# Fixed rotation of four score banks, and another order of score units, in an attention and mixture-of-experts kernel

## Chip, cores and metric

The kernel runs on one core of one Trainium2 chip. The metric is the device time of one execution in microseconds; less is better. Three runs of the kernel before took 604.11, 605.59 and 605.93 us, a median of 605.59.

## What is computed

A pre-norm transformer layer: causal attention with 16 heads of 8 values, then a mixture of 8 experts of which each token uses 2. The input is 8 sequences of 512 tokens with 128 values, all in float32.

```python
x = x + attn(layernorm(x))
x = x + moe(layernorm(x))

def attn(x):                        # b=8, t=512, H=16, HD=8
    q, k, v = (x @ Wq), (x @ Wk), (x @ Wv)      # split into heads
    s = einsum('bqhd,bkhd->bhqk', q * HD**-0.5, k)
    p = softmax(where(causal, s, -inf))
    return einsum('bhqk,bkhd->bqhd', p, v) @ Wo + bo

def moe(x):                         # E=8, F=512, TOPK=2
    probs = softmax(x @ gate_w.T)
    topk_probs, topk_idx = top_k(probs, 2)
    hidden = relu(einsum('th,ehf->tef', x, w1) + b1)
    all_out = einsum('tef,efh->teh', hidden, w2) + b2
    return sum(all_out[topk_idx] * topk_probs)
```

## The kernel before

The program is recorded by a set of Python generators ("lanes": setup, project, shifts, attend, route, experts, sums). Each yields a number, the point in time at which its next piece should be recorded, in units of one sequence; the lane with the least number goes on (L1351 to L1359). For PE, ACT, DVE and SP the order of recording is the order on the engine. So each of these engines works through one fixed list, and an instruction that waits holds up all behind it on its engine.

Attention computes its scores twice. A tile of scores is always 128 partitions by 512 float32, one PSUM bank.

The lane `shifts` (L557) finds the largest score of each row. For a group of four heads (two pairs of heads, `pr`) it goes through three kinds of unit, `S_UNITS` (L83): kind 0 has two banks, kind 1 two banks, kind 2 one. Each bank gets its causal blocks by bfloat16 matmuls (L597 for the blocks left of the diagonal, L602 for the diagonal one), and VectorE takes the maximum over it (L616) into `pm`. After the six units of a group, the maxima are combined and negated (`nm`, L622), split into two bfloat16 parts (`nh`, L632 and L633), and, two units into the next group, transposed by PE (`nmTp`, L562), copied by ACT (`nmT`, L564) and written by two POOL DMAs as two more rows of `q2` (L570). With those rows, the second pass gives scores from which the row's maximum has been taken.

The lane `attend` (L642) makes the second pass, key-major, some two groups behind `shifts` (LEAD, 0.55 of a sequence). `T_UNITS` (L88) has two kinds with two banks and one with one; per group there are six units, of 2, 2, 2, 2, 1 and 1 banks. Each bank is filled by L752 and L757 and read by one exp on ACT (L762) into `pt`. The exps are later multiplied by the values (`po`, L673). In the recorded order a unit of `attend` is followed by a unit of `shifts`, in turn; a group has ten banks of each. Other lanes put their work in between: projections of a later sequence (L446 to L458), norms and routing of an earlier one, and expert tiles (`ph` L1251, ReLU L1258 or L1260, `py` L1110, L1114).

PSUM has eight banks: `ps_sc` (L123) holds four for the scores of both passes, and, behind attention, for `ph` of the expert tiles; `ps_mm` three for everything else; `ps_o` one for `po`. In `ps_sc` all tiles carry one tag, so a new tile takes whichever of the four buffers the tile framework picks when the program is built. A tile's first matmul waits until the reader of the bank's last tile has finished.

Of the kernel before, what the change touches and what calls it, by code (L numbers as in the profile page):

```python
# [9 lines left out]
F32 = mybir.dt.float32  # L10
# [3 lines left out]
ALU = mybir.AluOpType  # L14
AX = mybir.AxisListType
PSUM = bass.MemoryType.PSUM
# [10 lines left out]
def preln_attn_moe(ctx: ExitStack, tc: tile.TileContext, x, wq, wk, wv, wo, bo,  # L27
# [57 lines left out]
        (((0, 0, 0), (0, 2, P)), ((1, 0, 0), (1, 2, P))),  # L85
        (((0, 1, 0), (1, 1, 2 * P)),),
    )
    T_UNITS = (  # L88
        (((0, 0, 0),), ((1, 0, 0),)),
        (((0, 1, 0), (0, 3, 3 * P)), ((1, 1, 0), (1, 3, 3 * P))),  # L90
# [29 lines left out]
    work = ctx.enter_context(tc.tile_pool(name="work", bufs=2))  # L120
    small = ctx.enter_context(tc.tile_pool(name="small", bufs=2))
    slots = ctx.enter_context(tc.tile_pool(name="slots", bufs=1, space=DRAM))
    ps_sc = ctx.enter_context(tc.tile_pool(name="ps_sc", bufs=4, space=PSUM))  # L123
    ps_mm = ctx.enter_context(tc.tile_pool(name="ps_mm", bufs=3, space=PSUM))
    ps_o = ctx.enter_context(tc.tile_pool(name="ps_o", bufs=1, space=PSUM))

# [129 lines left out]
    def in_order(ins):  # L256
        tc.keep_in_program_order(ins)
        if last_exp[0] is not None:
            tc.add_manual_dep(
                ins.ins, last_exp[0].ins.name,  # L260
                mybir.DependencyInfo(
                    mybir.DependencyClass.Sync, mybir.DependencyReason.DATA
                ),
                reason="indirect transfers keep the pace of attention",
            )

    def mm_tile(name):
        return ps_mm.tile([P, T], F32, tag="mm", name=name)
# [288 lines left out]
    def shifts():  # L557
        late = []

        def transposed(b, g, nh):  # L560
            pt = mm_tile(f"nmTp_{b}_{g}").bitcast(BF16)
            nc.tensor.transpose(pt[:, :P], nh, ident_bf)  # L562
            nmT = small.tile([32, P], BF16, tag="nmT", name=f"nmT_{b}_{g}")
            nc.scalar.copy(nmT, pt[:32, :P])  # L564
            late.append(lambda: rows(b, g, nmT))

        def rows(b, g, nmT):

            for l in range(2):
                ins = nc.gpsimd.dma_start(  # L570
                    out=q2_buf[b % 2][KS + l : KS + l + 1, HG * g : HG * g + HG],
                    in_=nmT[16 * l : 16 * l + 16],
                )
                if b > 0:
                    tc.keep_in_program_order(ins)
            shifted.add((b, g, 2))

        for b in range(B):
            for g in range(G):
                t0 = b - LEAD + g / G + (0.1 if b == 0 < g else 0.0)  # L580
                yield t0
                assert b in packed
                q2, k2 = q2_buf[b % 2], k2_buf[b % 2]

                pm = pm_buf[g % 2].rearrange("p (n u) t k -> p u n (t k)", u=2)
                for pr in range(2):
                    n = 2 * g + pr
                    for i, unit in enumerate(S_UNITS):
                        yield t0 + (3 * pr + i) / 24
                        for v, bank in enumerate(unit):  # L590
                            ps = ps_sc.tile(
                                [P, T], F32, tag="sc", name=f"s_{b}_{n}_{i}_{v}"
                            )
                            for u, t, at in bank:
                                h, q = 2 * n + u, ts(t, P)
                                if t > 0:
                                    nc.tensor.matmul(  # L597
                                        ps[:, at : at + t * P], lhsT=q2[:KS, h, q],
                                        rhs=k2[:KS, h, : t * P],
                                        start=(at == 0), stop=True, skip_group_check=True,  # L600
                                    )
                                nc.tensor.matmul(  # L602
                                    ps[:, at + t * P : at + (t + 1) * P],
                                    lhsT=q2[:, h, q], rhs=k2[:, h, q],
                                    start=(at + t == 0), stop=True, skip_group_check=True,
                                )
                            blocks = ps.rearrange("p (a q) -> p a q", q=P)
                            if i == 0:
                                top, src = pm[:, v, pr, 12:13], ps
                            elif i == 1:  # L610
                                top, src = pm[:, v, pr, 3:7], blocks
                            else:
                                top, src = pm[:, :, pr, 8], ps.rearrange(
                                    "p (u k) -> p u k", u=2
                                )
                            nc.vector.tensor_reduce(top, src, AX.X, ALU.max)  # L616
                        if t0 + (3 * pr + i) / 24 < 0:
                            keep_warm(WARM[2], f"{g}_{pr}_{i}")
                        if late:
                            late.pop(0)()  # L620
                nm = small.tile([P, HG * NT], F32, tag="nm", name=f"nm_{b}_{g}")
                nc.vector.tensor_reduce(  # L622
                    nm, pm_buf[g % 2].rearrange("p h t k -> p (h t) k"), AX.X, ALU.max,
                    negate=True,
                )
                nh = nh_buf[g % 2]
                nm = nm.rearrange("p (h o a) -> p h o a", o=2, a=2)
                hi, lo = (
                    nh[:, ts(l, HG * NT)].rearrange("p (h a o) -> p h o a", a=2, o=2)
                    for l in range(2)  # L630
                )
                V.tensor_copy(hi, nm)  # L632
                V.tensor_tensor(lo, nm, hi, ALU.subtract)  # L633
                if b > 0:
                    late.append(lambda: None)
                late.append(lambda b=b, g=g, nh=nh: transposed(b, g, nh))
        while late:
            late.pop(0)()
            yield B - LEAD + 0.05


    def attend():  # L642
# [90 lines left out]
        for b in range(B):  # L733
            for g in range(G):
                yield b + g / G
                assert (b, g, 2) in shifted
                q2, k2 = q2_buf[b % 2], k2_buf[b % 2]
                for i, unit in enumerate(T_UNITS):
                    pts = []
                    for pr in range(2):  # L740
                        yield b + g / G + (2 * i + pr + 0.5) / 24
                        n = 2 * g + pr
                        pt = work.tile(
                            [P, 2, T], F32, tag="pt", name=f"pt_{b}_{n}_{i}", bufs=6
                        )
                        for v, bank in enumerate(unit):
                            ps = ps_sc.tile(
                                [P, T], F32, tag="sc", name=f"st_{b}_{n}_{i}_{v}"
                            )
                            for u, j, at in bank:  # L750
                                h, k = 2 * n + u, ts(j, P)
                                nc.tensor.matmul(  # L752
                                    ps[:, at : at + P], lhsT=k2[:, h, k], rhs=q2[:, h, k],
                                    start=(at == 0), stop=True, skip_group_check=True,
                                )
                                if j < NT - 1:
                                    nc.tensor.matmul(  # L757
                                        ps[:, at + P : at + T - j * P],
                                        lhsT=k2[:KO, h, k], rhs=q2[:KO, h, (j + 1) * P :],
                                        start=False, stop=True, skip_group_check=True,  # L760
                                    )
                            last_exp[0] = nc.scalar.activation(pt[:, v, :], ps, AF.Exp, scale=SCALE)  # L762
                        pts.append(pt)
                        go_on()
                    products.append(lambda b=b, g=g, pts=pts, unit=unit, i=i: product(
                        b, g, pts, unit, i == 0, i == 2))
                attended.add((b, g))
# [279 lines left out]
    def experts():  # L1047
# [192 lines left out]
        for n, (s, i) in enumerate(tiles):  # L1240
            first, m = quad(s, i)
            yield when(s, i + 1)
            if after(s, i):
                ph = ps_sc.tile([P, T], F32, tag="sc", name=f"ph_{s}_{i}")
                hT = work.tile([P, 2, T], F32, tag="pt", name=f"hT_{s}_{i}", bufs=6)
                hT = hT[:, 0, :].rearrange("p (c t) -> p c t", c=FC)
            else:
                ph = mm_tile(f"ph_{s}_{i}")
                hT = work.tile([P, FC, P], F32, tag="hT", name=f"hT_{s}_{i}")
# [138 lines left out]
```

## Time and profile before

| | |
|---|---|
| median of three runs | 605.59 us |
| the profiled execution | 598.14 us |
| its span, first to last instruction | 596.4 us |
| mean granted TensorE clock | 0.954 |
| PE busy (share of the span) | 515.4 us (86%) |
| PE weight loads | 378.0 us (63%) |
| DVE | 430.9 us (72%) |
| ACT | 306.5 us (51%) |
| POOL | 220.2 us (37%) |
| L762, exp, 320 of 128x512 | 179.1 us, 600 ns each |
| L616, maximum, 320 of 128x512 | 206.0 us, 682 ns each |

Engines are PE (TensorE matmuls), PEld (its weight loads, which overlap them), DVE (VectorE), ACT (ScalarE), POOL (GpSimd) and SP (SyncE). Busy time is the time in which an instruction of the engine is in flight; matmuls are pipelined, so a new one may start while an older one's record still runs. Where a row has an arrow and a name behind idle time, that instruction's end is what released the waiting one. In names such as `pt<-st`, the left side is written and the right side read; L762 is line 762 of the kernel. Score matmuls of the first pass (tile `s`) run from 25.7 to 428.7 us, those of the second (tile `st`) from 44.9 to 462.5 us.

### The profile page before, as it was taken

To read this page: it belongs to the slowest core of one execution; us is meant where nothing else is said; L and a number is where in the kernel's file an instruction comes from. 1 tells how busy PE (TensorE), PEld (TensorE's weight loads), DVE (VectorE), ACT (ScalarE), POOL (GpSimd) and SP (SyncE) were. 2 spreads that over 40 slices of the span, in tenths; PEclk is the share of its full clock that TensorE was granted. 3 is DMA by queue.
4 is the path that set the end of the run, shared out by engine and by line. 5 is a ranking of instruction groups with operands and counts; after the bars stand their busy time and mean duration, and the time that the engine had idled before them with its cause. 6 is when DMAs were issued, how large, how long until landed. Compare 5 with 4: busy or idle time off the path is not lost. (4 is left out here: it accounts for less than half of the span.)

```text
span 596.4 us, 14010 instructions
## 1 busy us (share of the span) xinstructions
PE 515.4 (86%) x4762; PEld 378.0 (63%) x4762; DVE 430.9 (72%) x1367; ACT 306.5 (51%) x673; POOL 220.2 (37%) x278
## 2 busy tenths in 40 slices
PE   6979999988888988888799999998899788879980
PEld 4745455545445565665566777766576687879970
DVE  7788778898778977978788877797753354323694
ACT  2646656665645566465447465654454233345530
POOL 4032202315514422533443336335335334654441
PEclk9888899999979999999799999999999788999995
DMA  2568198188199455406502784322344586668783
GB/s 57 160 133 186 28 226 210 38 214 215 27 208 181 125 142 127 124 19 179 149 30 67 180 202 120 89 64 73 87 116 114 181 248 185 192 184 246 243 293 110
DMA packets 68762, 86.07 MB, mean 144 GB/s; under 512 B 11540, under 2 KB 50748, under 8 KB 66652
## 3 DMA queue, kind: packets, MB, share of 16 engines
q1 hardware_dynamic: 61508, 74.87, 49.1%
q0 software_dynamic: 6592, 9.65, 5.0%
q8 instruction: 39, 0.64, 0.5%
q10 hardware_dynamic: 592, 0.66, 0.4%
q14 instruction: 31, 0.25, 0.2%
HBM read 61.34 MB, written 26.16 MB: 147 GB/s over the span
## 5 line engine op out<-in xcount | busy, mean ns | idle before, releaser
L762 ACT ACTIVATE pt<-st 128x512 f32<-128x512 f32 x320 | 179.1, 600 | 128.1 <-PE st L752 58.3
L616 DVE TENSOR_REDUCE pm<-s 128x1 f32<-128x512 f32 (+2 forms) x320 | 206.0, 682 | 36.4 <-PE s L602 30.3
L1148 POOL DMA_INDIRECT ys<-yo,to x78 | 76.1, 975 | 125.4 <-ACT pt L762 50.2
L597 PE MATMUL s<-k,q 72*128 72x384 bf16 (+2 forms) x384 | 93.9, 280 | 16.0 <-ACT pt L762 12.8
L752 PE MATMUL st<-q,k 128*128 128x128 bf16 x512 | 92.9, 222 | 14.8 <-ACT pt L762 6.4
L602 PE MATMUL s<-k,q 128*128 128x128 bf16 x512 | 94.3, 223 | 7.4 <-ACT pt L762 5.5
L757 PE MATMUL st<-q,k 74*128 74x256 bf16 (+2 forms) x384 | 93.9, 280 | 0.0
L673 PE MATMUL po<-pt,va 128*18 128x512 f32 (+3 forms) x1024 | 92.5, 445 | 0.5 <-ACT pt L762 0.3
L1110 PE MATMUL py<-w_sb,hT 128*128 x624 | 88.6, 286 | 4.2 <-DVE yo L1114 2.0
L1016 POOL DMA_INDIRECT xs<-xn_f,slot x64 | 63.2, 987 | 64.1 <-ACT pt L762 35.7
L1110 PEld LDWEIGHTS py<-w_sb,hT 128*128 128x128 f32 x624 | 79.5, 199 | 8.2 <-issue 3.6
L602 PEld LDWEIGHTS <-q 128*128 128x128 bf16 x512 | 51.0, 100 | 37.7 <-issue 34.8
L570 POOL DMA_DIRECT2D q<-nmT x64 | 33.7, 529 | 76.4 <-ACT nmT L564 71.1
L597 PEld LDWEIGHTS <-q 72*128 72x128 bf16 x384 | 37.8, 100 | 36.5 <-issue 29.7
L752 PEld LDWEIGHTS <-k 128*128 128x128 bf16 x512 | 51.6, 101 | 6.3 <-issue 2.4
L757 PEld LDWEIGHTS <-k 74*128 74x128 bf16 x384 | 37.7, 98 | 26.2 <-issue 20.8
L673 PEld LDWEIGHTS po<-pt,va 128*18 128x18 f32 x1024 | 23.1, 97 | 29.6 <-issue 22.7
L1251 PE MATMUL ph<-xgT,wt 128*128 128x128 f32 x288 | 41.0, 286 | 0.8 <-ACT pt L762 0.8
L1251 PEld LDWEIGHTS ph<-xgT,wt 128*128 128x128 f32 x288 | 35.8, 195 | 5.7 <-issue 2.4
L1258 ACT ACTIVATE hT<-ph,q 128x128 f32<-128x128 f32 x72 | 21.0, 368 | 27.9 <-PE ph L1251 11.7
L1258 ACT ACTIVATE hT<-ph,wt 128x128 f32<-128x128 f32 x72 | 20.6, 367 | 22.3 <-issue 10.9
L456 POOL TENSOR_TENSOR part<-rest,part 128x512 bf16<-128x512 f32 x14 | 16.2, 1162 | 41.6 <-issue 33.8
(172 smaller groups left out, 688.0 us busy)
## 6 DMA issues: line engine op xcount, KB each, us to landing
wt<-wrows SPq DMA_DIRECT2D x36, 322.0 KB
k<-kparts SPq DMA_DIRECT2D x42, 192.0 KB
q<-wrows SPq DMA_DIRECT2D x24, 322.0 KB
k<-wrows SPq DMA_DIRECT2D x18, 322.0 KB
q<-qparts SPq DMA_DIRECT2D x30, 192.0 KB
q<-ys SPq DMA_DIRECT2D x15, 256.0 KB
k<-xs SPq DMA_DIRECT2D x42, 65.0 KB
qparts<-part SPq DMA_DIRECT2D x14, 192.0 KB
```

What stands on the lines that cost most here:

```text
L597: nc.tensor.matmul(ps[:, at : at + t * P], lhsT=q2[:KS, h, q], rhs=k2[:KS, h, : t * P], start=(at == 0), stop=True, skip_group_check=True,)
L602: nc.tensor.matmul(ps[:, at + t * P : at + (t + 1) * P], lhsT=q2[:, h, q], rhs=k2[:, h, q], start=(at + t == 0), stop=True, skip_group_che ...
L616: nc.vector.tensor_reduce(top, src, AX.X, ALU.max)
L673: nc.tensor.matmul(po[32 * h : 32 * h + 2 * VC, j * P :], lhsT=va[:, j, c0 : c0 + 2 * VC], rhs=at_cols(pts[pr], unit, u, at, W), start=(fi ...
L752: nc.tensor.matmul(ps[:, at : at + P], lhsT=k2[:, h, k], rhs=q2[:, h, k], start=(at == 0), stop=True, skip_group_check=True,)
L757: nc.tensor.matmul(ps[:, at + P : at + T - j * P], lhsT=k2[:KO, h, k], rhs=q2[:KO, h, (j + 1) * P :], start=False, stop=True, skip_group_c ...
L762: last_exp[0] = nc.scalar.activation(pt[:, v, :], ps, AF.Exp, scale=SCALE)
L1016: ins = nc.gpsimd.indirect_dma_start(out=xs[k], out_offset=bass.IndirectOffsetOnAxis(ap=slot[b][:, j * NT + i : j * NT + i + 1], axis=0), ...
L1110: nc.tensor.matmul(py, lhsT=hT[:, c, :], rhs=w2_sb[:, bass.ds(at[s, i] + c * E * D, D)], start=(c == 0), stop=(c == FC - 1),)
L1148: ins = nc.gpsimd.indirect_dma_start(out=ys[k], out_offset=bass.IndirectOffsetOnAxis(ap=to[s, first][:, i - first : i - first + 1], axis=0 ...
L1251: nc.tensor.matmul(ph[:, ts(c, P)], lhsT=wt[s, i][:, ts(c, P)], rhs=turned[s, first][:, ts(i - first, P)], start=True, stop=True,)
L1258: nc.scalar.activation(hT[:, c, :], ph[:, ts(c, P)], AF.Relu, bias=bias)
```

## The change

The pool of the score banks keeps four buffers, but as four tags of one buffer each, and a counter gives them out in turn: 1, 2, 3, 0, 1 and so on, over both passes and the expert tiles behind attention. The six units of a group in `shifts` are no longer recorded pair by pair (two banks, two, one, two, two, one) but in the order of `S_ORDER`, whose entries are (kind, pair): two banks, one, two, one, two, two. What each unit does is unchanged, and so are the points in time at which units are recorded.

```diff
+    S_ORDER = ((0, 0), (2, 0), (1, 0), (2, 1), (0, 1), (1, 1))
...
-    ps_sc = ctx.enter_context(tc.tile_pool(name="ps_sc", bufs=4, space=PSUM))
+    ps_sc = ctx.enter_context(tc.tile_pool(name="ps_sc", bufs=1, space=PSUM))
...
+    turn = [0]
+
+    def score_tile(name):
+        turn[0] = (turn[0] + 1) % 4
+        return ps_sc.tile([P, T], F32, tag=f"sc{turn[0]}", name=name)
...
-                for pr in range(2):
-                    n = 2 * g + pr
-                    for i, unit in enumerate(S_UNITS):
-                        yield t0 + (3 * pr + i) / 24
-                        for v, bank in enumerate(unit):
-                            ps = ps_sc.tile(
-                                [P, T], F32, tag="sc", name=f"s_{b}_{n}_{i}_{v}"
-                            )
+                for m, (i, pr) in enumerate(S_ORDER):
+                    n, unit = 2 * g + pr, S_UNITS[i]
+                    yield t0 + m / 24
+                    for v, bank in enumerate(unit):
+                        ps = score_tile(f"s_{b}_{n}_{i}_{v}")
...
-                            ps = ps_sc.tile(
-                                [P, T], F32, tag="sc", name=f"st_{b}_{n}_{i}_{v}"
-                            )
+                            ps = score_tile(f"st_{b}_{n}_{i}_{v}")
...
-                ph = ps_sc.tile([P, T], F32, tag="sc", name=f"ph_{s}_{i}")
+                ph = score_tile(f"ph_{s}_{i}")
```

More of the change, by code (lines that the diff above doesn't have):

```diff
@@ L585, in shifts @@
                 pm = pm_buf[g % 2].rearrange("p (n u) t k -> p u n (t k)", u=2)
-                for pr in range(2):
-                    n = 2 * g + pr
-                    for i, unit in enumerate(S_UNITS):
-                        yield t0 + (3 * pr + i) / 24
-                        for v, bank in enumerate(unit):
-                            ps = ps_sc.tile(
-                                [P, T], F32, tag="sc", name=f"s_{b}_{n}_{i}_{v}"
-                            )
[L594 to L600, printed above, removed]
-                                    )
[L602 to L605, printed above, removed]
-                                )
[L607 to L620, printed above, removed]
@@ new lines, in shifts @@
+                for m, (i, pr) in enumerate(S_ORDER):
[3 more added lines that the diff above has]
+                        ps = score_tile(f"s_{b}_{n}_{i}_{v}")
+                        for u, t, at in bank:
+                            h, q = 2 * n + u, ts(t, P)
+                            if t > 0:
+                                nc.tensor.matmul(
+                                    ps[:, at : at + t * P], lhsT=q2[:KS, h, q],
+                                    rhs=k2[:KS, h, : t * P],
+                                    start=(at == 0), stop=True, skip_group_check=True,
+                                )
+                            nc.tensor.matmul(
+                                ps[:, at + t * P : at + (t + 1) * P],
+                                lhsT=q2[:, h, q], rhs=k2[:, h, q],
+                                start=(at + t == 0), stop=True, skip_group_check=True,
+                            )
+                        blocks = ps.rearrange("p (a q) -> p a q", q=P)
+                        if i == 0:
+                            top, src = pm[:, v, pr, 12:13], ps
+                        elif i == 1:
+                            top, src = pm[:, v, pr, 3:7], blocks
+                        else:
+                            top, src = pm[:, :, pr, 8], ps.rearrange(
+                                "p (u k) -> p u k", u=2
+                            )
+                        nc.vector.tensor_reduce(top, src, AX.X, ALU.max)
+                    if t0 + m / 24 < 0:
+                        keep_warm(WARM[2], f"{g}_{pr}_{i}")
+                    if late:
+                        late.pop(0)()
@@ L746, in attend @@
                         for v, bank in enumerate(unit):
-                            ps = ps_sc.tile(
-                                [P, T], F32, tag="sc", name=f"st_{b}_{n}_{i}_{v}"
-                            )
+                            ps = score_tile(f"st_{b}_{n}_{i}_{v}")
                             for u, j, at in bank:
```

## The prediction

> **What bounds the kernel now.** First the table of busy time by stretch, split where attention's scores begin (45 us) and end (430 us) and where the last exp has run (463 us); columns are PE, PEld, DVE, ACT, POOL busy us, then granted clock:
>
> ```profile
> 45.00:430.00 385.00, 346.30 (x3412) 230.31 (x3410) 316.21 (x922) 221.05 (x454) 137.11 (x162) 0.97 0.52 127
> 430.00:463.00 33.00, 30.84 (x291) 23.35 (x283) 15.84 (x79) 17.36 (x43) 12.59 (x14) 1.00 0.44 120
> 463.00:597.00 134.00, 103.53 (x827) 98.87 (x827) 64.21 (x278) 47.14 (x151) 57.82 (x60) 0.89 0.69 209
> ```
>
> The change works in the first row, 385 us. PE looks 90% busy there, DVE 82% (316/385), ACT 57%. The chain of waits covers only the last 130 us (expert matmuls behind attention, which the change leaves alone), so I read the first stretch from the waits inside it:
>
> ```profile
> ACT pt L762 <- PE st L752: 55.3, 47, 2.9
> DVE pm L616 <- PE s L602: 25.8, 37, 1.8
> PE s L597 <- ACT pt L762: 12.8, 23, 2.4
> PE st L752 <- ACT pt L762: 6.4, 12, 1.0
> PE s L602 <- ACT pt L762: 5.5, 9, 1.6
> PE st L752 <- DVE pm L616: 3.3, 7, 1.0
> ```
>
> Columns: total us, times, longest. PE waits 24.7 us for exps (12.8+6.4+5.5, 44 times) and 5.1 us for maxima (with 0.9+0.9 of L597 and L602), and the readers wait for PE in turn. So PE, in program order, is the pacemaker, and what holds it up is a score bank that has not been read yet.
>
> These totals understate it, because a matmul's record is 0.22 us long while the next may start 0.06 us later: shorter holds don't show as idle. The timeline has one of each sort:
>
> ```profile
> 219.54 0.22 PE L757 MATMUL st<-q,k 74*128 74x128 bf16 x1
> ...
> 219.77 0.22 PE L602 MATMUL s<-k,q 128*128 128x128 bf16 x1
> 219.86 0.60 ACT L762 ACTIVATE pt<-st 128x512 f32<-128x512 f32 x1 [1.05 <-PE st L757]
> 220.51 0.22 PE L602 MATMUL s<-k,q 128*128 128x128 bf16 x1 [0.52 <-ACT pt L762]
> ```
>
> ```profile
> 160.39 0.22 PE L602 MATMUL s<-k,q 128*128 128x128 bf16 x1
> ...
> 160.64 0.69 DVE L616 TENSOR_REDUCE pm<-s 128x2 f32<-128x512 f32 x1 [0.59 <-PE s L602]
> ...
> 161.05 0.22 PE L602 MATMUL s<-k,q 128*128 128x128 bf16 x1
> 161.39 0.32 PE L597 MATMUL s<-k,q 72*128 72x384 bf16 x1
> ```
>
> From the last matmul into a bank to the first of its next tile takes 0.97 us through an exp (219.54 to 220.51) and 1.00 us through a maximum (160.39 to 161.39), with the reader idle. One bank of scores takes PE 0.22 us (a 384-column record is followed after 0.165, a 128-column one after 0.056). In the first case PE had one bank to fill in between and stood still from 219.83 to 220.51; in the second it lost 0.28 us (161.05+0.06 to 161.39) and the waits view shows nothing.
>
> **The holds, counted.** I laid the score tiles' bank addresses, as built, beside the records of L597, L602, L752, L757 and their readers L616, L762. A hold is a first matmul that starts later than the pitch of the matmul before it allows, within 0.15 us of its bank's read ending. Over the kernel they make 58.5 us: 44.9 behind exps, 13.6 behind maxima. Sorted by "cover", PE's bare matmul time between the two uses of the bank:
> behind exps, cover under 0.6 us: 87 uses, 40.3 us; longer cover: 239 uses, 4.6 us;
> behind maxima, cover under 0.8 us: 26 uses, 4.0 us; longer cover: 294 uses, 9.6 us.
>
> **Part one: banks in turn.** Before, of 678 reuses 6 come one score tile later (the second bank of a unit on the bank of its first), 87 two, 117 three, 265 four, 203 five to seven. After, the built program has 678 at four. Counting cover along its PE order, with the same pitches: exps 0 under 0.6 and 316 above; maxima 88 under 0.8 (all 0.67 to 0.74, three banks of 0.22) and 232 above. Prices of the long classes as measured, class by class: 6.2 us for exps, 8.4 us for maxima. The first class, 40.3 us, goes. What is new is that 88 times, not 26, PE meets a bank whose maximum has had only three banks of time.
>
> **The price of those 88** was bounded from three rows. Least: the 26 of before cost 4.0/26 = 0.15 us; but 20 of them had DVE idle (turnaround 1.00), having fallen there by choice. Most: the first maximum of most units ends on average 1.43 us after the last matmul into its bank started (records of L616 against L597/L602), so 1.43+0.05-0.06-0.67 = 0.75 us. Between: with DVE idle the first bank of a unit costs 1.00-0.06-0.67 = 0.27, and the second, whose maximum comes 0.61 after the first (two in 1.29 us) while PE needs only 0.22, another 0.39; mean 0.33. A third of first maxima start at once. I take 0.40, nearest to the idle case, because a PE held up by DVE gives DVE time to catch up. 88 x 0.40 = 35.2 us.
>
> Sum for the banks: 6.2 + 8.4 + 35.2 = 49.8 against 58.5: -8.7 us. With 0.15: 27.8, -30.7. With 0.75: 80.6, +22.1.
>
> **Part two: the order of units.** The same 10 banks, 28 matmuls and 10 maxima per group of four heads; the orders of ACT and SP do not change, PE's and DVE's only inside the score units. A group now ends on a two-bank unit: its second maximum ends about 0.61 us later, and with it nm and nh (L622 to L633). In the next group one bank fewer stands ahead of the transposition L562, 0.22 us. Queued behind that are the next exp tile's matmuls on PE. Its slack, from the end of nh to L562, was below 0.9 us in 7 of 32 groups (0.66, 0.15, 0.06, 0.06, 0.38, 0.65, 0.44). If all were lost that is 3.9 us; where PE waits for maxima anyway the two overlap. I take +2 (0 to 3.9). The row copies on POOL and the exps behind them have two groups of lead, the cover that keeps them free: some 25 us (L597 and L602 run from 25.7 to 428.9 us, 12.6 for each of 32 groups). Were that gone, the one wait of st for nmT's rows, 1.8 us, is the price.
>
> **The clock.** Granted clock is 0.66 in two 10-us stretches of attention (170 to 180, 290 to 300) and 1.00 nearly everywhere else there: some 3.4 us of PE time each. One more or one fewer moves the time by that much either way; it goes into the range.
> The Trainium skill, "TensorE: Matmul & The Clock Gate", section "A second HAM failure mode: psum-queue depth-cycling", speaks against the change: cycling through banks with small pauses between the matmuls made the clock swing between half and full. By the row nothing is added; by the rule, more such stretches, an estimate of one or two at the row's 3.4 us, which would turn the sum to about 0. No run here shows it yet.
>
> **The sum.** -8.7 + 2 = -6.7 us. On the profiled execution: 598.14 us (span 596.4 and 1.7 around it) becomes 591.4. The median of the three runs, 605.59, lies 7.45 above the profile; moved by the same amount it gives **598.9 us**.
>
> **Rivals.**
> 1. *DVE is the wrong engine to wait for* (slower). The waits move from ACT, 57% busy, to DVE, 82% busy. Three times a group (two before a score unit, one before the first exp tile) PE comes back 0.67 to 0.74 us after filling a bank that waits in DVE's queue behind norms, routing and ReLUs. For: mean end 1.43 us, and 1.97 for the unit that follows another closely. Against: the holds behind maxima are only 13.6 us now, and such a hold never leaves DVE idle. It decides from 58.5 = 14.6 + 2 + 88p, p = 0.48 us. At 0.60 it gives 605.59+10.9 = 616.5; at the bound 0.75, 629.7.
> 2. *The short waits cost little* (much faster): at the idle-DVE price for a first bank, 0.27, holds are 38.4: -20.1, 585.5; at 0.15 and no transposition loss, 574.9. For: the measured 0.15. Against: those uses were not placed blindly.
> 3. *Nothing comes through*: PE's gain is spent at the next thing in line (oqp, expert weights, DVE's 82%), 605.6.
> 4. *It doesn't do what it says*: excluded, the built addresses are at distance four throughout.
>
> **How the numbers follow.** Forecast 0.32 (own range 592 to 603), rival 2 0.20, rival 3 0.11, rival 1 0.37. Range: down to 582 (leaves out about half of rival 2's lower part, 0.07), up to 618 (leaves out a third of rival 1, 0.12). About 0.3%, 1.8 us, is what these runs can tell from no change. Faster 0.52, same 0.11, slower 0.37.
>
> **What would show it.** Right: PE's waits for exps fall from 24.7 us to under 5, the 0.52-like gaps after T tiles vanish, and waits of s and st on L616 rise from 5.1 us, not above 20; attention's last exp ends 5 to 10 us before 463. Wrong: waits for L616 above 30 us, or the end of attention unmoved while exp waits vanish (rival 3), or a third stretch at clock 0.66.

## The result, and the profile after

| | before | changed |
|---|---|---|
| median of 20 runs each, beside each other | 604.29 us (597.99 to 609.09) | 603.48 us (602.22 to 610.76) |
| mean of the 20 | 604.40 | 604.64 |
| ratio to before, 95% interval | | 1.007 (1.0041 to 1.010) |
| the profiled execution, its span | 598.14, 596.4 | 610.76, 609.0 |
| its mean granted clock | 0.954 | 0.933 |

The forecast gain of 6.7 us is not there. The ratio leaves out runs more than 1.5% above a kernel's fastest one, and as one run of before at 597.99 us puts that bar at 606.96, six of before's 20 fall out (607.16 to 609.09) and none of the changed kernel's, which is why the ratio says 0.7% slower where means and medians agree. Two later comparisons of the same changed kernel gave 0.995 (0.9893 to 1.0006) and 1.0045 (0.9996 to 1.0095), and before against itself 1.0035 (0.9986 to 1.0085). It is a change of nothing, or of some 2 us for the worse.

The table of busy time by stretch of the changed kernel, at the same bounds as before (us, then PE, PEld, DVE, ACT, POOL busy, granted clock, DMA share, GB/s):

```profile
45.00:430.00 385.00, 346.15 (x3358) 228.34 (x3359) 312.80 (x915) 215.67 (x448) 133.53 (x158) 0.96 0.52 125
430.00:463.00 33.00, 29.67 (x248) 21.70 (x248) 16.89 (x76) 15.78 (x37) 10.43 (x13) 0.84 0.37 101
463.00:597.00 134.00, 114.80 (x919) 107.62 (x917) 63.71 (x280) 52.62 (x162) 62.43 (x66) 0.93 0.68 208
```

In the first 385 us PE is as busy as before (346.15 against 346.30 us) but shows 3358 matmuls instead of 3412, so it runs late by some 50 matmuls, in part because of its clock (0.96 against 0.97). The second row has a clock of 0.84 where before had 1.00. In the third PE does 919 matmuls instead of 827: the end is the same work, met later.

PE's waits in attention (45 to 440 us) of the changed kernel; total us, times, longest:

```profile
PE st L755 <- DVE pm L621: 11.9, 33, 1.4
PE s L607 <- DVE pm L621: 10.1, 24, 1.1
PE s L602 <- DVE pm L621: 7.5, 11, 1.5
PE st L755 <- ACT pt L765: 1.9, 6, 0.5
PE nmTp L570 <- DVE nh L638: 1.6, 1, 1.6
```

L602, L607, L755 are the old L597, L602, L752; L621 is the maximum (old L616), L765 the exp (old L762), L570 the transposition (old L562). The change does what it says: waits for exps have gone from 24.7 to 1.9 us. What the first three lines say is where they went: 29.5 us behind maxima, from 5.1.

Counted with the shorter holds, as in the prediction (us that a first matmul of a score tile starts late behind its bank's reader):

| holds, us | behind exps | behind maxima | all |
|---|---|---|---|
| before, first profile and second | 44.9, 44.6 | 13.6, 14.8 | 58.5, 59.4 |
| changed, three profiles | 4.6, 5.0, 3.9 | 52.0, 52.5, 53.1 | 56.6, 57.5, 56.9 |

Nearly all that was saved behind exps is paid again behind maxima. One such hold, in the timeline of the changed kernel (start, duration, both us; in brackets the idle time before, and what ended it):

```profile
184.75 0.34 PE L602 MATMUL s<-k,q 72*128 72x384 bf16 x1
...
184.93 0.22 PE L607 MATMUL s<-k,q 128*128 128x128 bf16 x1
...
185.01 0.18 DVE L638 TENSOR_TENSOR nh<-nm,nh 128x16 bf16<-128x16 f32 x1
185.10 0.16 DVE L929 TENSOR_SCALAR have<-pc 128x8 int32<-128x8 f32 x1
...
185.67 0.22 PE L570 MATMUL nmTp<-ident_bf,nh 128*128 128x128 bf16 x1
...
186.43 0.17 DVE L956 TENSOR_TENSOR steps<-begins 128x8 f32<-128x8 f32 x1
186.51 1.28 DVE L621 TENSOR_REDUCE pm<-s 128x1 f32<-128x512 f32 x2
...
187.19 0.60 ACT L765 ACTIVATE pt<-st 128x512 f32<-128x512 f32 x1 [2.81 <-PE nmTp L570]
187.25 0.22 PE L755 MATMUL st<-q,k 128*128 128x128 bf16 x1 [1.36 <-DVE pm L621]
```

PE fills the bank by 184.93, fills three more, does a transposition at 185.67 and is back at the bank in turn. Its maximum has not begun: on DVE, routing's small operations (L929 to L956, 0.15 to 0.21 us each) stand ahead of it until 186.51. PE stands still until 187.25, with everything behind it. In this hold no other bank would have served: the other three are read out later, one by the exp at 187.19 (until 187.79), two by maxima (until 187.79 and 189.04). In others one would. Comparing, at each hold behind a maximum, the ends of the reads of all four banks gives 23.5, 24.6 and 24.2 us in the three profiles of the changed kernel, of 52 to 53, that went by after another bank was free; in before it is 1 us of 14 to 15.

### The profile page after: what moved, and what is told of

Same layout as the page of the kernel before. It is cut to its first block, busy times and chain, and to the rows that moved or that the text cites. A ratio compares the mean times of both kernels' runs of the same rounds, so it can differ in the third digit from the quotient of the medians.

```text
span 609.0 us, 14013 instructions
## 1 busy us (share of the span) xinstructions
PE 526.6 (86%) x4762; PEld 383.2 (63%) x4762; DVE 430.8 (71%) x1367; ACT 304.8 (50%) x673; POOL 220.1 (36%) x278
## 4 chain that ended last, share of the span: by engine, by line
PE 50%; DVE 32%; issue 7%; ACT 5%; DMA 3%; POOL 1%; SPq 1%; another core or an unknown queue 0%; POOLq 0%; ACTq 0%; DVEq 0%
DVE pm L621 16%; PE py L1113 11%; PE ph L1254 10%; PE po L678 9%; PE st L760 4%; PE st L755 3%; PE s L602 3%; PE s L607 2%; PE pq L454 2%; ACT k L251 2%; PE xgTp L1213 2%; PE oqp L699 1%; PE pl L804 1%; ACT hT L1261 1%; DVE hT L1263 1%
## 5 line engine op out<-in xcount | busy, mean ns | idle before, releaser
L765 ACT ACTIVATE pt<-st 128x512 f32<-128x512 f32 x320 | 178.0, 599 | 142.0 <-PE st L760 62.3
L621 DVE TENSOR_REDUCE pm<-s 128x1 f32<-128x512 f32 (+2 forms) x320 | 206.5, 683 | 38.1 <-PE s L607 35.0
L755 PE MATMUL st<-q,k 128*128 128x128 bf16 x512 | 93.0, 225 | 17.5 <-DVE pm L621 11.9
L607 PE MATMUL s<-k,q 128*128 128x128 bf16 x512 | 96.1, 225 | 11.1 <-DVE pm L621 10.2
L602 PE MATMUL s<-k,q 72*128 72x128 bf16 (+2 forms) x384 | 94.0, 282 | 10.3 <-DVE pm L621 7.5
L678 PE MATMUL po<-pt,va 128*18 128x512 f32 (+3 forms) x1024 | 95.9, 458 | 2.5 <-ACT pt L765 2.5
L760 PE MATMUL st<-q,k 74*128 74x256 bf16 (+2 forms) x384 | 95.7, 285 | 0.0
L1113 PE MATMUL py<-w_sb,hT 128*128 x624 | 89.9, 289 | 4.5 <-issue 1.8
L1113 PEld LDWEIGHTS py<-w_sb,hT 128*128 128x128 f32 x624 | 81.2, 202 | 9.1 <-issue 5.1
L607 PEld LDWEIGHTS <-q 128*128 128x128 bf16 x512 | 50.9, 101 | 34.5 <-issue 32.0
L602 PEld LDWEIGHTS <-q 72*128 72x128 bf16 x384 | 38.6, 101 | 39.2 <-issue 32.9
L755 PEld LDWEIGHTS <-k 128*128 128x128 bf16 x512 | 52.5, 103 | 7.1 <-DMA q<-nmT 1.6
L1261 ACT ACTIVATE hT<-ph,q 128x128 f32<-128x128 f32 x72 | 21.0, 368 | 24.7 <-PE ph L1254 12.2
L1261 ACT ACTIVATE hT<-ph,wt 128x128 f32<-128x128 f32 x72 | 20.6, 368 | 25.4 <-issue 13.4
L1254 PE MATMUL ph<-xgT,q 128*128 128x128 f32 x192 | 27.4, 290 | 6.2 <-issue 5.4
```

The lines of the kernel that those rows point to most:

```text
L602: nc.tensor.matmul(ps[:, at : at + t * P], lhsT=q2[:KS, h, q], rhs=k2[:KS, h, : t * P], start=(at == 0), stop=True, skip_group_check=True,)
L607: nc.tensor.matmul(ps[:, at + t * P : at + (t + 1) * P], lhsT=q2[:, h, q], rhs=k2[:, h, q], start=(at + t == 0), stop=True, skip_group_che ...
L678: nc.tensor.matmul(po[32 * h : 32 * h + 2 * VC, j * P :], lhsT=va[:, j, c0 : c0 + 2 * VC], rhs=at_cols(pts[pr], unit, u, at, W), start=(fi ...
L755: nc.tensor.matmul(ps[:, at : at + P], lhsT=k2[:, h, k], rhs=q2[:, h, k], start=(at == 0), stop=True, skip_group_check=True,)
L760: nc.tensor.matmul(ps[:, at + P : at + T - j * P], lhsT=k2[:KO, h, k], rhs=q2[:KO, h, (j + 1) * P :], start=False, stop=True, skip_group_c ...
L1113: nc.tensor.matmul(py, lhsT=hT[:, c, :], rhs=w2_sb[:, bass.ds(at[s, i] + c * E * D, D)], start=(c == 0), stop=(c == FC - 1),)
```

## The experiments

The time of one execution follows the clock that it was granted. In the 277 runs of the twelve programs below that ran on like chips, a line with one slope for all gives -4.65 us (± 0.16) for each 0.01 of mean clock, with 2.15 us of scatter left. So beside each median and ratio stands the time at a clock of 0.95, read from that line with its standard error; before is 602.3 ± 0.2 there, and the changed kernel 604.1 ± 0.3. From chip to chip before itself reads 601.9 to 602.8 there, so a difference under 1 us between programs that ran on different chips says nothing.

### The two kernels again, and each part alone

The changed kernel and before were run again, unaltered.

> The changed kernel, once more, because its first profile fell on its slowest execution (610.8 against a median of 603.5). Theory A: holds 57 us again, attention's last exp ends within 3 us of before's 463 once half-clock time is taken off. Theory B: half-clock time between 45 and 480 us clearly above before's 27 us (35 or more) in this profile too. If it is near 27 us, the clock of the first profile was chance, and the time should be within 2 us of before's at the same clock.

> The kernel before, once more, for its second profile and its clocks. Theory A (the sum of holds decides): ratio 1.000 within 0.3%, holds 58 us as in the first profile. Theory B (the half-clock time decides): the same ratio, and the runs' times order themselves by their mean clock, about 6 us for each 0.01 of clock; half-clock time between 45 and 480 us is near the 27 us of its first profile, well under the 44 us of the changed kernel.

Measured: 605.1 us (12 runs) and 603.56 (12), beside 604.09 for before (35). The slices of the granted clock, in tenths, each a fortieth of the span; first the changed kernel as profiled first, then again:

```profile
PEclk9877999999977999999899999999789789989995
```

```profile
PEclk9987999999989999989989999999999989989995
```

The first has six slices at 7, the second one. Half-clock stretches cost, at half their length, 22.2, 13.7 and (a third profile) 18.8 us inside the changed kernel's attention, 10.2 and 5.1 in before's. But over all runs the mean clock is 0.9497 for the changed kernel (45 runs) and 0.9477 for before (116): the profiled executions are no fair sample, and the 12.6 us between the first two spans is their clock (41.8 against 28.7 us lost to half clock, 13.1 us).

The third look at the changed kernel, later, gave the ratio 1.0045 of above and holds of 56.9 us.

> The changed kernel on the same chip, for the open remainder of 1.6 us at equal clock. Holds 57 us as in both profiles. Theory A: within 0.3% of before. If turns cost something beside holds, 0.3 to 0.5% slower than before here too.

*Rotation alone*, with the old order of units:

```diff
-    S_ORDER = ((0, 0), (2, 0), (1, 0), (2, 1), (0, 1), (1, 1))
+    S_ORDER = ((0, 0), (1, 0), (2, 0), (0, 1), (1, 1), (2, 1))
```

> Banks strictly in turn, units of scores in the old order (pair by pair). Short covers behind maxima 74 instead of 88, none behind exps. Theory A: holds about 50 us (74 at 0.405, the longer ones at the prices of the changed kernel's profile), so 1% faster than before and than the changed kernel: the order of units is what spoils the rotation. Theory B: long waits for maxima remain, half-clock time as in the changed kernel; ratio to before 1.000 to 1.01.

Measured: 608.13 us (12 runs), ratio 1.0075 (1.0035 to 1.0116), 606.2 ± 0.6 at clock 0.95. The 1% gain that theory A expected, with some 50 us of holds, is not there: the holds are 59.5 us. Its waits for maxima:

```profile
PE s L602 <- DVE pm L621: 16.3, 19, 1.8
PE s L607 <- DVE pm L621: 7.3, 14, 1.6
PE st L755 <- DVE pm L621: 3.8, 21, 0.2
```

*Order alone*, with the pool choosing among four banks:

```diff
-    ps_sc = ctx.enter_context(tc.tile_pool(name="ps_sc", bufs=1, space=PSUM))
+    ps_sc = ctx.enter_context(tc.tile_pool(name="ps_sc", bufs=4, space=PSUM))
...
-        return ps_sc.tile([P, T], F32, tag=f"sc{turn[0]}", name=name)
+        return ps_sc.tile([P, T], F32, tag="sc", name=name)
```

> Units of scores in the new order, banks given out as before by the pool (84 short covers behind exps, 25 behind maxima, against 87 and 26). Theory A: holds 57 to 60 us, within 0.5% of before. Theory B: the same, with half-clock time as before's (27 us between 45 and 480). Rival C (the later second maximum of a group and the transposition behind it cost time): 2 to 4 us slower than before, with waits of nmTp for nh above 3 us.

Measured: 601.65 us (13 runs), ratio 0.9938 (0.9894 to 0.9981), 600.9 ± 0.6 at clock 0.95, with holds of 54.3 us, below the 57 to 60 that were expected. Its waits are those of before:

```profile
PE st L755 <- ACT pt L765: 11.0, 18, 1.8
PE s L607 <- ACT pt L765: 10.4, 15, 2.9
PE st L755 <- DVE pm L621: 4.0, 7, 1.4
```

What follows: the parts add, within their errors, and each went the other way than predicted. Rotation costs 3.9 us in the old order (602.3 to 606.2) and 3.2 in the new one (600.9 to 604.1); the order saves 1.4 and 2.1. The holds agree in sign, not fully in size: rotation 58.5 to 59.5 and 54.3 to 56.6; order 58.5 to 54.3 and 59.5 to 56.6. Under rotation the new order's saving shows at L602, first matmul of most units: 16.3 us in the rotation alone, 7.5 in the changed kernel. Why the order saves was not taken apart further.

### Is the speed of the maximum what counts?

Both kernels with maxima over half of the columns:

```diff
-                            top, src = pm[:, v, pr, 12:13], ps
+                            top, src = pm[:, v, pr, 12:13], ps[:, : T // 2]
...
-                            top, src = pm[:, v, pr, 3:7], blocks
+                            top, src = pm[:, v, pr, 3:7], blocks[:, :, : P // 2]
...
-                            )
+                            )[:, :, :P]
```

> The kernel before, with each maximum taken over half of its bank's columns (the other half is left out; key 0 of each block is kept). A maximum should take 0.42 us instead of 0.68. Theory A (time follows the holds): holds behind maxima fall from 14 to about 4 us, those behind exps stay at 45, so 8 to 12 us faster than before. Theory D (DVE's 82% is what sets attention's pace): 320 x 0.26 = 83 us less DVE work, 20 us faster or more. Theory B (half-clock time decides): follows its clock, a few us either way.

> The changed kernel with the same half-length maxima (the other half of each bank's columns is left out). Turnaround through a maximum falls to 0.74 us, against a cover of 0.67 to 0.74. Theory A: the 52 us of holds behind maxima fall to 10 to 15, all holds to 15 to 20, so it is 25 to 35 us faster than before_half. Theory D: both half kernels equal within 5 us. Theory E (a hold behind a maximum costs nothing, since DVE goes on working and PE catches up): equal to before_half as well, although its holds are 30 us less.

The maxima of the changed kernel, and of the same kernel with half of the columns (ns: least, median, most):

```profile
L621 DVE TENSOR_REDUCE pm<-s x320: 656/681/694, 25.8 to 436.1; 128x1 f32<-128x512 f32 x64, 128x4 f32<-128x512 f32 x64, 128x2 f32<-128x512 f32 x32
```

```profile
L621 DVE TENSOR_REDUCE pm<-s x320: 391/415/428, 26.6 to 404.3; 128x1 f32<-128x256 f32 x64, 128x4 f32<-128x256 f32 x64, 128x2 f32<-128x256 f32 x32
```

Measured: before with half maxima 574.61 us, 0.9555 (0.9509 to 0.9601); changed with half maxima 575.59, 0.9558 (0.9503 to 0.9614); beside 601.99. Some 83 us less of DVE work (206.5 to 122.7) are worth 27.4 and 26.4 us of the median (20 and 23 at clock 0.95, where the two stand at 582.1 and 581.5 ± 0.9). These are the outcomes that were written down for theory D, that DVE's work sets the pace: 20 us or more for before, and the two halved kernels equal within 5 us. Theory A, that time follows the holds, had 8 to 12 us for before and a further 25 to 35 us between the two, and missed both. Afterwards the holds fit too: they fell from 56.6 to 27.7 in the changed kernel (short covers from 0.41 to 0.15 us each), but in before from 58.5 to 32.5 as well. Its holds behind exps, which the edit does not touch, fell from 44.9 to 21.1 us: the pool chooses again when the program is built, and with quicker maxima it leans less on banks with an exp (39 reuses come two tiles later, where it was 87). So the edit takes away holds and DVE work together, and doesn't tell which of them the time follows: 20 and 23 us are three quarters of the holds that went (26.0 and 28.9 us), and a quarter of the DVE work.

### One bank more

The rotation over five banks, with one taken from the pool for everything else:

```diff
-    ps_mm = ctx.enter_context(tc.tile_pool(name="ps_mm", bufs=3, space=PSUM))
+    ps_mm = ctx.enter_context(tc.tile_pool(name="ps_mm", bufs=2, space=PSUM))
...
-        turn[0] = (turn[0] + 1) % 4
+        turn[0] = (turn[0] + 1) % 5
```

> The changed kernel with five score banks in turn and two instead of three for everything else on PE. Shortest cover behind a maximum rises from 0.67 to 0.89 us (68 uses at 0.89, none under 0.8). Theory A: holds behind maxima fall from 52 to 20 to 30 us, a gain of 20 us or more, less what the two remaining general banks cost in new waits of pq, py, ph, xgTp and oqp. Theory E: no gain, and slower by those new waits.

Measured: 614.57 us (6 runs), ratio 1.0192 (1.0129 to 1.0255), 615.3 ± 0.9 at clock 0.95. Cover is now at least 0.89 us and the holds fall to 38.8 us (36.8 behind maxima, half of them at L755), 18 us less than with four:

```profile
PE st L755 <- DVE pm L621: 18.8, 41, 1.5
```

Yet PE stands idle in attention (each matmul counted until the next may start, half-clock stretches left out) for 134.6 us against 125.8: the expert matmuls into `py`, left with two general banks, wait 10.2 us where they waited 2.8. More cover does shrink the holds; the bank they were bought with was worth more. The wait for `py` is only the largest of the new ones: the time rises by 11 us at equal clock though the holds fell by 18, and where the rest is lost was not traced. The outcome, no gain and slower by new waits, is the one written down for theory E, that a hold behind a maximum costs nothing; what the other kernels say to that stands in the part on why the prediction was wrong.

### Choosing the bank

Four tags as in the changed kernel, but at each tile the bank that should be free first. The code that records the program adds up busy time of PE, DVE and ACT, with durations from the profile:

```diff
-        turn[0] = (turn[0] + 1) % 4
-        return ps_sc.tile([P, T], F32, tag=f"sc{turn[0]}", name=name)
+        i = min(range(4), key=lambda n: free_ns[n])
+        at_ns["PE"] = max(at_ns["PE"], free_ns[i])
+        free_ns[i] = float("inf")
+        return ps_sc.tile([P, T], F32, tag=f"sc{i}", name=name), i
+
+    def score_read(i, key):
+        at_ns[key] = max(at_ns[key], at_ns["PE"] + 250) + 560.0
+        free_ns[i] = at_ns[key] + 120
```

`score_read` is called after each maximum ("DVE") and exp ("ACT"); `at_ns` also grows with every other matmul, DVE and ACT operation as it is recorded. It ran in the new order three times, and once in the old.

> The changed kernel's order of units, the four banks given out by a count kept while recording: each new tile takes the bank that PE, ACT and DVE, at the durations of the profile, free first. Short covers: 56 behind exps (before 87), 34 behind maxima (the changed kernel 88). Theory A: holds about 35 to 40 us (56 at 0.35, 34 at 0.2, the longer ones 8 to 12), so 15 us faster than either kernel. Theory B or E: within 0.5% of order_only.

> The kernel aware once more, for an interval (its first six runs had a mean of 596.8 against 604.4 for 58 runs of the kernel before, and its holds 51 us against 58.5). Theory A (time follows holds, one for one): 1% faster than before, ratio 0.985 to 0.995. If the first result was its clock (0.9555 against 0.946), the ratio is 0.995 to 1.0.

> aware on the same chip as aware_relu_b and a_third. Theory A: holds 7 to 8 us below before's, so 0.5 to 1% faster than before and than the changed kernel on this chip too.

> Banks by the count kept while recording, units in the old order. Short covers 53 behind exps and 42 behind maxima (with the new order 56 and 34). Theory A with additive parts: the new order was worth 2 us at equal clock with the pool's banks, so this is 1 to 3 us slower than aware_b and still 1 to 5 us faster than before. If the count of recording is what gains, it equals aware_b.

PE's waits of the first (a helper records the operations, so all carry its line L276):

```profile
PE st L276 <- DVE pm L276: 8.4, 15, 1.8
PE st L276 <- ACT pt L276: 7.0, 13, 1.9
PE s L276 <- ACT pt L276: 6.7, 13, 1.4
PE s L276 <- DVE pm L276: 6.1, 11, 1.0
```

The waits are shared between the two readers. Holds are 51.3 us (25.9 behind maxima, 25.4 behind exps) in the new order, 53.1 in the old. Times: 597.4 (6 runs); 596.64 (12), 0.9954 (0.991 to 0.9998); 603.98 (12), 0.9945 (0.987 to 1.002); in the old order 598.36 (12), 0.9967 (0.9924 to 1.0011). At clock 0.95: 599.9 ± 0.4 and 599.1 ± 0.6, 4 to 5 us under the changed kernel and 2 to 3 under before. A choice beats the turn; the new order adds nothing to a choice. Theory A's 35 to 40 us of holds and its 15 us of time did not come: short covers behind maxima, taken at 0.2 us, cost about 0.3 here, and 7.2 us of holds less than before go with 2.4 us of time.

### Less work ahead of the maxima

During attention every other ReLU of the expert tiles ran on DVE; here all of them run on ACT:

```diff
-                if c < FC - 1 if after(s, i) else n % 2 == 0:
+                if c < FC - 1 or not after(s, i):
```

> The kernel before, with every ReLU of an expert tile inside attention on ACT (64 of 0.34 us leave DVE between 226 and 463 us, ACT takes as many of 0.37): 18 us less on DVE, some 23 us more on ACT. Theory F (the price of a short cover behind a maximum is DVE's backlog): its 14 us of holds behind maxima lose 2 to 4 us, its 45 behind exps gain 2 to 6, because exps queue behind the ReLUs: within 0.5% of before.

> The changed kernel with the same ReLUs on ACT. Theory F: the 88 short covers fall from 0.41 toward the 0.33 of an idle DVE in the second half of attention, and the holds at longer cover by a third: 5 to 10 us fewer holds behind maxima, none more behind exps (all covers there are over 0.6), so 4 to 10 us faster than the changed kernel and than before_relu. If the cover alone sets the price (turnaround against cover, DVE idle or not): no change against the changed kernel.

> The kernel aware with all ReLUs of attention's expert tiles on ACT: both gains at once. Theory F (a hold's price is the cover less the reader's backlog, and the two edits act on different holds: the bank choice on which reuses are short, the ReLUs on how late DVE is): they add, holds 45 to 48 us (aware 50.6, ReLU on ACT worth 4), 3 to 5 us faster than aware, 1 to 1.5% faster than before. If both take away the same holds (a bank choice that looks at DVE's queue has already avoided its backlog): no faster than aware or before_relu alone, ratio 0.995 to 0.997.

> aware_relu again, now beside aware and the changed kernel on one chip, since its first runs fell on a chip on which the kernel before takes 576 us instead of 602. Holds were 49.8 us, aware's 50.0 to 51.3: if time follows holds, it equals aware within 2 us; if ReLUs on ACT bring DVE time that holds don't show, it is 3 to 5 us faster than aware.

| kernel | holds without, with the edit, us | at clock 0.95 without, with, us | ratio to before |
|---|---|---|---|
| before | 58.5, 54.8 | 602.3, 598.1 ± 0.6 | 0.996 (0.9919 to 1.0001) |
| changed | 56.6, 52.6 | 604.1, 600.7 ± 0.6 | 0.9966 (0.992 to 1.0012) |
| bank chosen, new order | 51.3, 49.8 and 50.6 | 599.9, 596.9 ± 0.9 | 1.0035 (0.9974 to 1.0095) and 0.9848 (0.9772 to 0.9924) |

In the first two rows 3.7 and 4.0 us of holds go with 4.2 and 3.4 us of time, but here too with some 18 us less DVE work. In before the holds moved against theory F: those behind exps fell by some 7 us and those behind maxima rose by 3, as the pool chose again. In the changed kernel it is the maxima that gain: a short cover costs 0.35 instead of 0.41 us. The last row was measured twice (its 596.9 is from the second alone): on a chip on which before takes 575.66 us it gained nothing (574.73), and beside a before of 604.39 it took 590.86 us (6 runs), the best version here. The stretch of attention in that profile:

```profile
45.00:430.00 385.00, 344.98 (x3474) 229.94 (x3472) 308.95 (x897) 235.94 (x517) 138.48 (x164) 1.00 0.53 128
```

3474 matmuls are done by 430 us where before had 3412, with 15 us more on ACT and 7 less on DVE; its clock of 1.00 helps as well. Of the 3 us it gains at equal clock over the chosen bank alone, the holds explain about 1; the rest is open.

## Why the prediction was wrong

*That the holds are what PE loses*: held up in part. Holds behind exps fell by 40 us, those behind maxima rose by 38, and the time stood still: the two kinds cost about the same. What a microsecond of holds costs shows best in the six kernels that do the same DVE work with four score banks (before, changed, rotation alone, order alone, bank chosen in either order): they have 51.3 to 59.5 us of holds and take 599.1 to 606.2 us at clock 0.95, and a line through them has a slope of 0.7 (± 0.2). So DVE's work alone doesn't set the time (theory D), and holds behind maxima are not free (theory E); but before lies 2 us under the line, and a single difference can come out at a third (order alone: 4.2 us of holds, 1.4 of time) or at one for one (rotation alone to bank chosen, old order: 6.4 and 7.1). And the count sees only score banks, as the fifth bank showed.

*Exps, 44.9 to 6.2 us*: right, 4.6, 5.0 and 3.9. (The prediction's 87 + 239 reuses behind exps are more than the 320 exps there are; at 0.02 us for a use of the longer class, nothing hangs on it.)

*"I take 0.40 ... 88 x 0.40 = 35.2 us"*: right in size, though 0.40 was picked between bounds. The 88 short covers cost 35.6, 36.2 and 36.1 us, 0.41 each; placed by the turn alone in the old order, 0.43 each (74 uses). Rival 2's price, 0.15 to 0.27, holds only where the pool chose the bank (0.15 to 0.22 in before and in the order alone), not where the count kept while recording did (about 0.3).

*"Prices of the long classes as measured, class by class: ... 8.4 us for maxima"*: this is the step that failed. The 232 longer covers cost 16.4, 16.3 and 16.9 us. Their prices came from before, where the pool rarely took a bank while another was free sooner; given out in turn, a bank comes back whether or not its maximum has run. The reads of all four banks show this: of the longer covers behind maxima (counted from 0.76 us, 14.7 to 15.5 us of holds) 7.6 to 8.1 us in the three profiles of the changed kernel went by after another bank was free; in before 0.6 to 0.7 us of 10.5. That is the size of the miss. I had seen for the short covers that the pool's picks are not blind ("those uses were not placed blindly") and did not apply it to the long ones. With 16.4 in place of 8.4 the sum is 4.6 + 16.4 + 35.6 = 56.6, -1.9 instead of -8.7.

*The order, +2*: the wait that was named is there but half as long: PE is late at the transposition by 2.6 and 3.2 us instead of 2.0 and 2.2 (without half-clock stretches), about +1. That the order by itself shortens holds by 3 to 4 us was not seen, as I only counted what it delays.

So the two terms as measured give about -1.9 + 1 = -1 us: nothing that can be told from no change. Of the rivals, "nothing comes through" (605.6) gave the time, and its sign came true: exp waits vanished and the end of attention did not move. With half-clock cost taken off, the last exp ends at 455.9, 455.2 and 457.0 us, and at 453.3 and 456.9 in before. That rival had the gain spent at the next thing in line, DVE among others; it was spent on the same banks, behind DVE. PE's idle time in attention without half-clock stretches is 125.8 and 128.1 us, against 125.2 and 128.5 before. This is rival 1's mechanism, DVE as the wrong engine to wait for, at a price of (52.0 - 8.4)/88 = 0.50 if all is put on the 88 uses, just over the 0.48 from which it was to decide.

*"Such a hold never leaves DVE idle"*: refuted. The chain of waits of the changed kernel (start, us, what) runs through one:

```profile
431.42 1.06 POOL rstd_f L370
432.50 0.35 DVE xn_f L379
432.85 0.60 DVE pm L621
```

In its timeline:

```profile
431.82 0.22 PE L607 MATMUL s<-k,q 128*128 128x128 bf16 x1
...
432.50 0.35 DVE L379 TENSOR_SCALAR xn_f<-x,mv_f,rstd_f 128x128 f32<-128x128 f32 x1 [2.17 <-POOL rstd_f L370]
...
432.76 0.69 DVE L621 TENSOR_REDUCE pm<-s 128x2 f32<-128x512 f32 x1
...
433.51 0.32 PE L602 MATMUL s<-k,q 72*128 72x384 bf16 x1 [1.46 <-DVE pm L621]
```

DVE idles 2.17 us for a norm from POOL with a maximum queued behind it (its scores were in by 429.9 us), and PE, whose bank that is, idles with it.

*The signs to look for.* Waits for exps under 5 us: yes, 1.9. Waits for maxima not above 20: no, 29.5, just under the 30 that would have refuted me outright. Last exp before 463 us: no, 478.1, 468.8 in the next profile; part of that is the clock. A third stretch at low clock: in the profile yes, over the runs no. The Trainium skill ("TensorE: Matmul & The Clock Gate", section "A second HAM failure mode: psum-queue depth-cycling") tells of a kernel whose clock swung between half and full while it cycled through banks. Here the clock swings in both kernels, and over the runs no more under rotation: the mean is 0.9497 with it and 0.9477 without, though the three profiles of the changed kernel happen to have more half clock than the two of before.

*What stays open.* At equal clock the changed kernel is 1.8 us slower than before (604.1 ± 0.3 against 602.3 ± 0.2), while holds and transposition say 1 us faster; and the rotation costs 1 to 3 us more than its holds say (0.9 in the new order, 2.9 in the old). Three ratios of 0.995, 1.0045 and 1.007 do not settle whether that is the kernel or the sample of runs. Nor was it taken apart how much of the 20 us that half maxima bring is DVE's work itself rather than the holds.

## What to carry to other kernels

Buffers given out in turn remove the waits of bad picks and with them the good ones: a price of a reuse that is read from a schedule that chose its buffers belongs to that choice. Here the price of the longer covers doubled when the choice went. Ask which engine's list the waits move to; from one that is 57% busy to one that is 82% busy they came back here at the same size. Where the program is recorded in one order, counting busy time while recording and taking the bank that frees first gave 2 to 3 us here, and taking small work out of the list ahead of the reader 3 to 4.

## What the runs showed of the hardware

The clock decides more than the change. The same program took 593.6 to 615.2 us (before, 116 runs). In attention half clock comes in stretches of 3.4, 6.8 or 10.2 us, each behind 3.4 us in which PE paused. In two profiles of before and three of the changed kernel, cut into the 3.4 us steps of the clock's records, the 25 stretches follow steps in which PE was busy for 29 to 65% of the time; every step at full clock under 58% was followed by half clock, and none over 65%. In the table by stretch of the changed kernel, around the hold shown last:

```profile
428.60:432.00 3.40, 2.57 (x23) 1.11 (x22) 1.70 (x6) 1.45 (x3) 3.08 (x5) 1.00 0.14 45
432.00:435.40 3.40, 1.71 (x16) 1.26 (x15) 2.90 (x8) 1.19 (x3) 1.59 (x2) 1.00 0.51 115
435.40:445.60 10.20, 10.13 (x63) 6.83 (x63) 3.95 (x17) 4.18 (x10) 1.02 (x2) 0.50 0.31 86
445.60:449.00 3.40, 3.40 (x31) 2.35 (x30) 2.29 (x13) 3.02 (x8) 0.00 (x0) 1.00 0.03 7
```

PE works 1.71 of 3.4 us, with the wait of 1.46 us in them, and the next 10.2 us run at 0.50, a loss of some 5 us.

One chip ran the kernel before in 575.66 us (17 runs) where the others took 602 to 604.4, at a clock of 0.962: by the slope above that clock explains about 7 of the 27 us or so. The rest is open.
